# A two-layer mixture-of-experts network: shared experts moved, a softmax sum dropped, count stores on one queue

## The chip, the cores and the metric

The kernel runs on one core of a Trainium2 chip. A core has a matrix engine (PE, its weight loads shown as PEld), a vector engine (DVE), an activation engine (ACT), a general engine (POOL), a queue engine that only issues transfers (SP), and 16 DMA engines that all transfers share. Every engine works through its own instructions in order; semaphores order them between engines. The metric is the device time of one execution in microseconds (us).

## The reference

All values are float32. The input is 8192 tokens of 256 features (16 x 512 x 256). Four sublayers, each a layer norm and a residual sum: softmax attention, a mixture of experts (MoE), a recurrent attention with a forget gate, and the same MoE with the same weights again. The MoE is where the change lies:

```python
logits = x @ router_w.T                       # 64 experts
probs = softmax(logits)
topk_w, topk_ids = top_k(probs, 8)
topk_w = topk_w / sum(topk_w)                 # over the 8 chosen
# every token goes to its 8 experts; an expert takes its first 128 tokens
# in token order, later ones are dropped for it
pos = cumsum(onehot(topk_ids)) - 1
valid = pos < 128
# routed expert e, on its 128 tokens:
y = (silu(xb @ w_gate[e]) * (xb @ w_up[e])) @ w_down[e]        # 256 -> 192 -> 256
routed = sum over a token's valid experts of topk_w * y
# shared expert, on all tokens:
gu = x @ ws_gate_up
shared = (silu(gu[:, :192]) * gu[:, 192:]) @ ws_down
return routed + shared
```

## The kernel before

Tokens are worked on in 16 blocks of 512; a block is four chunks of 128 tokens, one token per partition. The profiled execution passes through these stages: attention of layer one (0 to 1378 us; the first MoE's block work is threaded into it, step by step, by the tables `dense` and `routed`, L425 to L450), the remainder of that block work and the first routed experts (to 1675), the forget attention (to 2151), the block loop of the second MoE (to about 2372), its routed experts (to 2627) and the last sum, `joined` (to 2672).

The order on each engine is written out: inside `manual_schedule` the instructions of PE, DVE, ACT, POOL and SP keep the order in which the program makes them. Transfers of a queue engine go through eight completion slots in turn, so that an issue can also wait for the landing of an older transfer that held its slot.

Class `Part` (L1388) holds the block work of one MoE. For block b: `normed` normalises the tokens and stores them to a DRAM table `rows` (L1520), from which the experts gather later; `features` transposes them to `xnT`; `logits` and `exps` give the unnormalised softmax `pr`; `choose` divides `pr` by its sum (its piece 0, L1564 to L1566), finds the eight largest (MAX8 and MATCH_REPLACE8, L1574 and L1575), and takes the chosen weights divided by their own sum, `wt` (L1581 to L1588); `count` transposes the 0/1 choice and makes a running count per expert with a scan, `cum` (L1596 to L1604). `added` and `counted` then store the counts to DRAM (L1607) and read them back as one row per chunk into the tile `cw` (L1493). The last block's counts go straight from tile to tile by four small transfers, `straight` (L1497 to L1501), alternately on SP and ACT.

The shared expert of a block is `gu` (12 PE passes into three banks, L1619), `silu` in two halves (a tanh on ACT, L1005, and two operations on DVE, L1006 and L1007, for each half), and `down` (16 PE passes, L1650, two copies on ACT, L1657, and one store of 512 KB by SP to the DRAM tensor `routed`, L1659). In the second MoE these run three blocks behind the choice (`lag = 3`, L1253 to L1273): iteration b does `gu` and `silu` of block b - 3 and `down` of block b - 4. In iterations 2 to 6 SP also fetches expert weights for five pairs of experts (`fetch`), 1.18 MB each time. The last three blocks' shared work lies behind the loop (L1275 to L1296), between the pieces of `place`, which turn the counts into token lists: `chunks_before` copies the last column of all counts into `after` (L1057), a product with a triangle sums the chunks (L1059), and for each pair of experts PE and DVE find the tokens (L1074 to L1103).

A routed expert e is: POOL gathers its 128 rows, `xe` (L1121, six experts ahead); PE transposes them (L1132), multiplies with the expert's weights (L1151) and after tanh and products with the down weights (L1175); ACT scales the result by the token's weight, `ye` (L1183); POOL adds it by an accumulating scatter to a DRAM tensor (L1186), even experts to `out`, odd ones to `routed`. Two tensors allow the next scatter to go while the last one lands. Weights come in pairs of experts into slots (11 pairs in the second MoE), POOL clearing each new slot once (L1465). At the end `joined` adds `routed` to `out` with eight accumulating transfers of 1 MB from POOL (L1369).

Of the kernel before, what the change touches and what calls it, by code (L numbers as in the profile page):

```python
# [17 lines left out]
P = 128  # L18
# [19 lines left out]
class Block:  # L38
# [129 lines left out]
    def attention(self, x, x1, wqkv, wo, rope, part, later):  # L168
# [11 lines left out]
        with ExitStack() as c:  # L180
# [270 lines left out]
            def each(s):  # L451

                n, i = divmod(s, CB)
                yield groups, n, weighted, i
                yield groups, n + 2, largest, i
                if i == 0:
                    yield groups, n - 1, summed
                    yield groups, n + 3, turn, kTs, H, "kT"
                if i == 1:
                    yield groups, n - 1, heads  # L460
                    yield groups, n + 1, row
                    yield groups, n + 3, turn, qTs, 0, "qT"
                b, at = divmod(s, steps)
                for work, far, *args in dense.get(at, []) + routed.get(at, []):

                    if b + far < z - 2 or work not in (part.shared, part.down):
                        yield self.nblk, b + far, work, *args

            with tc.manual_schedule(
# [540 lines left out]
    def routed(self, part, loads=False):  # L1010
# [9 lines left out]
        with ExitStack() as c:  # L1020
# [177 lines left out]
            with tc.manual_schedule(  # L1198
# [5 lines left out]
                    nc.sync.engine,  # L1204
                }
            ):
                nb, lag, ahead = self.nblk, 3, 6
                finds = {0: find(0, 2), 2: find(2, 2)}
                gathered = iter(range(E))

# [40 lines left out]
                    fetch(n)  # L1251

                if loads:  # L1253
                    for b in range(-4, nb + 1):
                        run(b + 4, nb, load)
                        if b == -3:
                            part.begin(nc.scalar)
                        run(b, nb, choose)
                        run(b + 2, nb, lambda b: part.normed(b, xs.pop(b)))
                        run(b + 1, nb, part.features)  # L1260
                        run(b - lag, nb, gu)
                        run(b - lag, nb, silu)
                        run(b + 1, nb, part.logits)
                        run(b + 1, nb, part.likely)
                        run(b, nb, part.count)
                        run(b, nb, counts)
                        run(b - 1 - lag, nb, down)
                        run(b + 1, nb, part.exps)
                        run(b + 3, nb, lambda b: part.moments(b, xs[b]))
                        if 2 <= b < 7:  # L1270
                            fetch(b - 2)
                        if b == nb:
                            chunks_before()  # L1273
                            place(0, 3)

                    begun, done, z = 5, 0, nb - 1
                    place(0, 2)
                    gather_to(1)
                    place(2, 3)
                    part.gu(z - 1, 0)  # L1280
                    place(2, 1)
                    part.gu(z - 1, 1)
                    place(2, 1)
                    gather_to(3)
                    silu(z - 1)
                    part.down(z - 2, 0)
                    part.down(z - 2, 2)
                    place(4, 3)
                    part.gu(z, 0)
                    place(4, 1)  # L1290
                    part.gu(z, 1)
                    place(4, 1)
                    gather_to(5)
                    silu(z)
                    down(z - 1)
                    down(z)  # L1296
                else:
                    begun, z = 8, nb - 1
                    room = part.own.enter_context(
# [38 lines left out]
                    place(8, 3)  # L1338
                    done = 2
                part.own.close()  # L1340
                part.slots(part.pairs - len(part.slot), "left")

                rest = [(n, piece) for n in range(begun, E // 2) for piece in range(4)]
                due, last = len(rest), E - 10
                for e in range(done - 2, E):
                    if e + ahead > 5:
                        run(e + ahead, E, gather_to)
                    place((e + 10) // many * many, 2 if (e + 10) % many == 0 else 1)
                    run(e + 2, E, turned)
                    run(e + 2, E, lastly)  # L1350
                    run(e + 1, E, widened)
                    run(e, E, narrowed)
                    while rest and (due - len(rest)) * last < due * (e + 1):
                        n, piece = rest[0]
                        if e < 2 * (n - part.pairs) + 3:
                            break
                        if piece == 0:
                            held(n)
                        part.fetch(*rest.pop(0))


    def joined(self, out, y):
# [25 lines left out]
class Part:  # L1388
# [3 lines left out]

    def __init__(self, ctx, k, x, y, weights, room, pairs, side):
        rw, self.w_gate, self.w_up, self.w_down, ws_gu, ws_down = weights
        self.ctx, self.pairs, self.slot, self.ws = ctx, pairs, [], {}
        self.k, self.nc, self.x, self.y, self.room = k, k.nc, x, y, room
        tc, T = k.tc, k.T
        self.own = ctx.enter_context(ExitStack())  # L1400
# [21 lines left out]
        self.bank = None  # L1422
        self.shared_weights = (rw, ws_gu, ws_down)

    def begin(self, queue):
        rw, ws_gu, ws_down = self.shared_weights
        nc, T, w = self.nc, self.k.T, self.pools[1]
        self.rw_sb = w.tile([P, KD, E], F32, name="rw_sb")
        queue.dma_start(out=self.rw_sb, in_=rw.rearrange("(k p) f -> p k f", p=P))

        self.wsg_sb = w.tile([P, KD, 2 * FF], F32, name="wsg_sb")
        for to, of, n in ((0, 0, FF), (FF, FF + P, FT), (2 * P, FF, P)):
# [7 lines left out]
        queue.dma_start(out=self.wsd_sb[0:FT, 1, :], in_=ws_down[P:FF, :])  # L1440

        self.hidden = []
        for i in range(self.room["hT"]):
            hT = w.tile([P, 2, BLK], F32, name=f"hT{i}")
            nc.gpsimd.memset(hT[FT:P, 1, :], 0.0)
            self.hidden.append(hT)
        for z in (self.rows, self.x, self.y):
            queue.dma_start(out=z[T : T + P, :], in_=self.k.zeros[:, 0 : z.shape[1]])


    def slots(self, n, side):
# [45 lines left out]
    def straight(self, b):  # L1497

        for i in range(CB):
            at, queue = b * CB + i, (self.nc.sync, self.nc.scalar)[i % 2]  # L1500
            queue.dma_start(out=self.cw[at : at + 1], in_=self.cum[:, ts(i, P)])  # L1501

    def tile(self, name, shape):
        return self.pools[self.room[name]].tile(shape, F32, name=name)
# [55 lines left out]
    def choose(self, b, piece):  # L1560
        nc, small, pr = self.nc, self.k.small, self.prs[b]
        if piece == 0:
            sm = small.tile([P, CB], F32, name="sm")
            nc.vector.tensor_reduce(sm, pr, AX.X, ALU.add)  # L1564
            nc.vector.reciprocal(sm, sm)
            nc.vector.tensor_tensor(  # L1566
                pr, pr, sm.unsqueeze(2).to_broadcast([P, CB, E]), ALU.mult
            )
            self.tops[b] = small.tile([P, CB, TOPK], F32, name="top")
            self.rests[b] = self.tile("rest", [P, CB, E])  # L1570
            return
# [39 lines left out]


    def gu(self, b, piece):
        nc, xnT = self.nc, self.xnTs[b]
        gu = self.gus[b, piece] = {}
        for m in ((0, 2), (1,))[piece]:
            gu[m] = self.bank()
            for kd in range(KD):
                nc.tensor.matmul(  # L1619
                    gu[m],  # L1620
                    lhsT=self.wsg_sb[:, kd, ts(m, P)],
                    rhs=xnT[:, kd, :],
                    start=(kd == 0),
                    stop=(kd == KD - 1),
                )
        if piece == 1:
            del self.xnTs[b]

    def silu(self, b, piece):
        if piece == 0:  # L1630
            self.hTs[b] = self.hidden[b % len(self.hidden)]
        gu = self.gus.pop((b, piece))
        high = (P, FT)[piece]
        gate = gu[piece][0:high]
        up = gu[2] if piece == 0 else gu[1][FT:P]
        th = self.tile("th", [P, BLK])[0:high]
        self.k.silu(self.hTs[b][0:high, piece, :], gate, up, th, 0.5)
# [5 lines left out]
    def down(self, b, i, pool=None):  # L1643
# [1 line left out]
        if i == 0:  # L1645
            self.ys[b] = (pool or self.pools[self.room["y"]]).tile([P, CB, D], F32, name="y")
        py = self.bank()
        for k in range(2):
            for m in range(2):
                nc.tensor.matmul(  # L1650
                    py[:, ts(k, D)],
                    lhsT=hT[:, m, ts(i + k, P)],
                    rhs=self.wsd_sb[:, m, :],
                    start=(m == 0),
                    stop=(m == 1),
                )
        nc.scalar.copy(self.ys[b][:, i : i + 2, :], py.rearrange("p (c d) -> p c d", c=2))  # L1657
        if i > 0:
            nc.sync.dma_start(  # L1659
                out=self.y[ts(b, BLK), :].rearrange("(c p) d -> p c d", p=P),  # L1660
                in_=self.ys.pop(b),
            )
            del self.hTs[b]


@with_exitstack
def hybrid_block_kernel(
# [27 lines left out]
    moe = (router, w_gate, w_up, w_down, ws_gu, ws_down)  # L1695
    later = k.forget_bias(b_bqk)
    with ExitStack() as c:
        part = Part(c, k, attended, routed, moe, ROOM, 13, "left")
        k.attention(x, attended, a_wqkv, a_wo, rope, part, later)
        k.routed(part)  # L1700
    k.forget_attention(
        attended, routed, out, (b_wqk, k.bqk_sb, b_wv, b_bv, b_wf, b_bf, b_wo, b_bo)
    )
    with ExitStack() as c:
        part = Part(c, k, out, routed, moe, ROOMY, 11, "left")
        k.routed(part, loads=True)
    k.joined(out, routed)

# [70 lines left out]
```

## Time and profile before

| what | value |
|---|---|
| device time, three runs | 2680.56, 2671.54, 2667.5 us; median 2671.54 |
| the profiled execution | 2674.27 us, span 2672.4 us |
| granted PE clock, mean | 0.95 |
| busy over the span | PE 92%, DVE 69%, ACT 48%, POOL 32% |
| transport | 226.48 MB, mean 85 GB/s |

The span is the time from the first to the last recorded instruction; the execution's own time has some two microseconds around it. A busy PE is not PE at its peak, since ends of matmuls are modelled. A group's line reads: line, engine, operation, output and input tile with their shapes, count, then busy time and mean duration in ns, then the idle time of the engine just before and what ended it. "x12" on a timeline's row means that twelve like instructions are drawn together. A trailing q (SPq, ACTq) is the engine's sequencer, which waits and issues transfers.

### The profile page before, as it was taken

The page shows a single profiled execution, that of the slowest core. Times are in us where ns is not written, and L with a number is a line of the kernel's source. Part 1 is how long each engine was busy: PE and PEld are TensorE (multiplying, and loading weights), DVE is VectorE, ACT ScalarE, POOL GpSimd, SP SyncE. Part 2 cuts the span into 40 slices and gives each one's busy share as a digit, 9 for nine tenths or more (in the row PEclk, how much of TensorE's full clock was granted, in tenths as well). Part 3 has the DMA queues.
Part 4 walks back from the last instruction along what each step waited for, and adds up shares of the span by engine and source line. Part 5 has one row for each costly group of instructions (what it writes and reads, how often), then busy time and mean ns, then how long its engine had stood idle before and what let it go on. Part 6 is the DMA issues. An engine that isn't in the chain of part 4 may idle for free.

```text
span 2672.4 us, 47696 instructions
## 1 busy us (share of the span) xinstructions
PE 2452.1 (92%) x17864; PEld 1517.9 (57%) x17864; DVE 1849.9 (69%) x4677; ACT 1293.0 (48%) x2654; POOL 845.6 (32%) x835
## 2 busy tenths in 40 slices
PE   6999999999999999999997886799999969998881
PEld 3444555445554455544446776567767656667771
DVE  6666667766777667776645664789889869966660
ACT  1656556565565655656542332466656523323330
POOL 3222212122121221212014776332332122117773
PEclk7999999999999999999898998899999969999996
DMA  1000111001110011100057887201111058739987
GB/s 57 2 17 19 35 37 35 21 21 35 37 35 21 21 35 37 35 21 13 27 151 207 237 229 156 90 29 58 60 53 53 21 146 185 175 106 258 246 220 148
DMA packets 210003, 226.48 MB, mean 85 GB/s; under 512 B 34286, under 2 KB 202222, under 8 KB 208750
## 3 DMA queue, kind: packets, MB, share of 16 engines
q1 hardware_dynamic: 180366, 174.43, 22.7%
q0 software_dynamic: 25728, 46.15, 8.7%
q8 instruction: 143, 2.34, 0.4%
q10 hardware_dynamic: 3680, 2.85, 0.3%
q14 instruction: 86, 0.70, 0.1%
HBM read 146.50 MB, written 84.48 MB: 86 GB/s over the span
## 4 chain that ended last, share of the span: by engine, by line
PE 76%; DVE 9%; DMA 7%; issue 3%; POOL 2%; ACT 1%; SPq 0%; ACTq 0%; POOLq 0%; DVEq 0%
PE sc L329 20%; PE sc L379 9%; DMA xe<-rows,token 5%; PE sc L255 4%; PE pb L797 4%; PE sc L1619 3%; PE sc L318 3%; PE sc L829 2%; PE sc L299 2%; PE sc L402 2%; PE sc L1650 2%; PE pb L861 2%; PE pb L906 2%; PE pb L722 2%; PE sc L1151 2%
## 5 line engine op out<-in xcount | busy, mean ns | idle before, releaser
L343 DVE TENSOR_REDUCE mx<-sc 128x1 f32<-128x512 f32 x1024 | 635.8, 684 | 375.5 <-PE sc L329 375.5
L369 ACT ACTIVATE pT<-sc 128x512 f32<-128x512 f32 x1024 | 528.6, 602 | 179.5 <-PE sc L329 179.5
L329 PE MATMUL sc<-qT,kT 17*128 17x512 f32 x2048 | 315.6, 646 | 0.0
L329 PE MATMUL sc<-kT,qT 16*128 16x512 f32 x2048 | 312.5, 609 | 1.5 <-DVE mx L343 1.4
L104 POOL TENSOR_SCALAR va<-mv 128x4 f32<-128x4 f32 x64 | 14.7, 230 | 756.6 <-DVE mv L98 742.8
L379 PE MATMUL sc<-pT,v 128*32 128x512 f32 x2048 | 241.8, 614 | 0.0
L846 DVE SCALAR_TENSOR_TENSOR pT<-sc,of,left 128x256 f32<-128x256 f32 x512 | 204.9, 474 | 23.2 <-PE sc L829 21.9
L329 PEld LDWEIGHTS sc<-kT,qT 16*128 16x128 f32 x2048 | 159.6, 189 | 94.3 <-issue 51.9
L277 POOL TENSOR_TENSOR t<-qk,rope_sb 128x512 f32<-128x512 f32 x62 | 78.8, 1271 | 404.1 <-ACT qk L263 396.9
L1121 POOL DMA_INDIRECT xe<-rows,token x128 | 131.0, 1023 | 96.8 <-DVE token L1103 39.7
L379 PEld LDWEIGHTS sc<-pT,v 128*32 128x32 f32 x2048 | 61.3, 112 | 173.1 <-issue 123.0
L329 PEld LDWEIGHTS sc<-qT,kT 17*128 17x128 f32 x2048 | 93.8, 184 | 90.0 <-issue 46.2
L255 PE MATMUL sc<-wqkv_sb,feat 128*128 128x512 f32 x256 | 128.0, 625 | 0.0
L144 ACT COPY oT<-sc 128x512 f32<-128x512 f32 x64 | 37.6, 587 | 169.4 <-PE sc L379 169.4
L797 PE MATMUL pb<-feat,wqk_sb 128*128 128x512 f32 x256 | 119.0, 598 | 0.0
L1186 POOL DMA_INDIRECT routed<-ye,token x64 | 101.9, 1592 | 41.2 <-ACT th L1160 10.4
L96 DVE BATCH_NORM_STATS2 bn<-x 128x6 f32<-128x256 f32 x256 | 89.1, 412 | 15.5 <-DMA x<-out 12.4
L318 PEld LDWEIGHTS sc<-ident,pad 128*128 128x128 f32 x512 | 54.8, 142 | 74.1 <-issue 38.9
L318 PE MATMUL sc<-ident,pad 128*128 128x128 f32 x512 | 86.1, 291 | 5.1 <-POOL pad L293 3.0
L285 POOL TENSOR_TENSOR t<-qk,rope_sb 128x256 f32<-128x256 f32 x124 | 90.7, 753 | 0.0
L1619 PE MATMUL sc<-xnT,wsg_sb 128*128 128x512 f32 x192 | 89.3, 603 | 0.0
L255 PEld LDWEIGHTS sc<-wqkv_sb,feat 128*128 128x128 f32 x256 | 45.8, 194 | 76.3 <-issue 38.3
(220 smaller groups left out, 4822.2 us busy)
## 6 DMA issues: line engine op xcount, KB each, us to landing
ws<-in_w_gate SPq DMA_DIRECT2D x64, 384.0 KB
ws<-in_w_up SPq DMA_DIRECT2D x64, 384.0 KB
rows<-xn SPq DMA_DIRECT2D x32, 512.0 KB
routed<-y SPq DMA_DIRECT2D x32, 512.0 KB
ws<-in_w_down SPq DMA_DIRECT2D x64, 256.0 KB
x<-in_x SPq DMA_DIRECT2D x16, 512.0 KB
attended<-x SPq DMA_DIRECT2D x16, 512.0 KB
ws<-in_w_down SPq DMA_DIRECT2D x64, 128.0 KB
```

The lines of the kernel that those rows point to most:

```text
L255: nc.tensor.matmul(pq, lhsT=xnTs[b][:, kd, ts(i, P)], rhs=wqkv_sb[:, kd, 0 : 2 * D], start=(kd == 0), stop=(kd == KD - 1),)
L285: eng.tensor_tensor(t2[:, :, lo : lo + HD // 2], qk2[:, :, :, 1 - half], rope_sb[:, i, HD + lo : HD + lo + HD // 2] .unsqueeze(1) .to_broa ...
L318: nc.tensor.transpose(pt[:, ts(i, P)], pads[b % 2][i][:, at : at + 4, :].rearrange("p h d -> p (h d)"), self.ident,)
L329: nc.tensor.matmul(scs[j], lhsT=lhs[at : at + high, ts(i, P)], rhs=rhs[at : at + high, :], start=True, stop=True,)
L343: nc.vector.tensor_reduce(mxs[n][:, j, i : i + 1], sc, AX.X, ALU.max, negate=True)
L369: nc.scalar.activation(pT[:, j, :], sc, AF.Exp, scale=float(HD) ** -0.5)
L379: nc.tensor.matmul(pav[ts(j, HP), :], lhsT=vs[b % 2][:, i, 4 * hg + j, :], rhs=pT[:, j, :], start=(i == 0), stop=(i == CB - 1),)
L797: nc.tensor.matmul(pq, lhsT=wqk_sb[:, kd, ts(m, P)], rhs=xnTs[b][:, kd, :], start=(kd == 0), stop=(kd == KD - 1),)
L846: nc.vector.scalar_tensor_tensor(pTs[n][:, :, ts(s8, HD)], sc[:, :, ts(s8, HD)], of[:, s8 : s8 + 1], here, ALU.mult, ALU.mult,)
L1121: nc.gpsimd.indirect_dma_start(out=xes[e], out_offset=None, in_=rows, in_offset=bass.IndirectOffsetOnAxis(ap=token[:, e : e + 1], axis=0),)
L1186: nc.gpsimd.indirect_dma_start(out=accs[e % 2], out_offset=bass.IndirectOffsetOnAxis(ap=token[:, e : e + 1], axis=0), in_=ye, in_offset=No ...
L1619: nc.tensor.matmul(gu[m], lhsT=self.wsg_sb[:, kd, ts(m, P)], rhs=xnT[:, kd, :], start=(kd == 0), stop=(kd == KD - 1),)
```

## The change

Five edits go together.

1. `choose` no longer divides by the softmax sum, in both MoEs. The chosen weights are divided by their own sum anyway, so the sum cancels.
2. In the second MoE the shared experts of blocks 3, 7 and 11 (`put_off`) leave the block loop. A generator, `between`, computes them in 24 pieces between the routed experts of e = 0 to 55: it loads the shared weights again (SP), loads the block's normalised rows from `rows` (SP), transposes them, and does the products in a pool of its own, `r_o`. A piece's second half (copies, tanh, products) follows at the start of the next expert. The results stay in three tiles until `paid` adds them to `out` with three accumulating transfers of 512 KB, ahead of `joined`. Since nothing else writes those blocks' rows of `routed`, `begin` clears them with twelve transfers of 128 KB on ACT's queue.
3. The other 13 blocks' shared work is cut into pieces with costs 4, 2, 2 and 2 and handed out evenly over the iterations (`shares`), from block 0 in iteration 0 on, in place of the fixed lag of three. Costs of 20 of 130, two blocks, are left for behind the loop.
4. `straight` issues its four transfers on ACT's queue alone, in both MoEs.
5. The second MoE has nine slots for pairs of weights instead of eleven.

```diff
@@ dense and routed tables of attention
-                    if b + far < z - 2 or work not in (part.shared, part.down):
+                    if work not in (part.shared, part.down) or (
+                        b + far < z - 2 and b + far not in part.put_off
+                    ):
@@ second layer's loop
-                    for b in range(-4, nb + 1):
+                    own = [b for b in range(nb) if b not in part.put_off]
+                    def first_part(b):
+                        part.gu(b, 0)
+                        part.silu(b, 0)
+                    def second_part(b):
+                        part.gu(b, 1)
+                        part.silu(b, 1)
+                    pieces = []
+                    for n, b in enumerate([*own, None]):
+                        if b is not None:
+                            pieces.append((4, b, first_part, b))
+                        if n > 0:
+                            pieces.append((2, own[n - 1], part.down, own[n - 1], 0))
+                            pieces.append((2, own[n - 1], part.down, own[n - 1], 2))
+                        if b is not None:
+                            pieces.append((2, b, second_part, b))
+                    total, spent = 10 * len(own), 0
...
+                    for b in range(-4, nb):
                         run(b + 4, nb, load)
                         if b == -3:
                             part.begin(nc.scalar)
                         run(b, nb, choose)
                         run(b + 2, nb, lambda b: part.normed(b, xs.pop(b)))
                         run(b + 1, nb, part.features)
-                        run(b - lag, nb, gu)
-                        run(b - lag, nb, silu)
+                        shares((total - 20) * (b + 1) // nb, b)
                         run(b + 1, nb, part.logits)
                         run(b + 1, nb, part.likely)
                         run(b, nb, part.count)
                         run(b, nb, counts)
-                        run(b - 1 - lag, nb, down)
                         run(b + 1, nb, part.exps)
                         run(b + 3, nb, lambda b: part.moments(b, xs[b]))
                         if 2 <= b < 7:
                             fetch(b - 2)
-                        if b == nb:
-                            chunks_before()
-                            place(0, 3)
-                    begun, done, z = 5, 0, nb - 1
+                    begun, done = 5, 0
+                    shares(total - 10)
+                    chunks_before()
+                    place(0, 3)
+                    shares(total - 8)
                     place(0, 2)
                     gather_to(1)
                     place(2, 3)
-                    part.gu(z - 1, 0)
...
+                    shares(total - 6)
+                    place(2, 2)
                     gather_to(3)
...
                     place(4, 3)
...
+                    shares(total - 4)
+                    place(4, 2)
                     gather_to(5)
+                    shares(total)
@@ routed experts
                 part.own.close()
+                filler = part.between("left") if part.put_off else iter(())
+                next(filler, None)
                 part.slots(part.pairs - len(part.slot), "left")
+                all_pieces, begun_pieces, open_piece = 8 * len(part.put_off), 0, False
...
                 for e in range(done - 2, E):
+                    if open_piece:
+                        next(filler, None)
+                        open_piece = False
...
                     run(e, E, narrowed)
+                    if e >= 0 and begun_pieces * (E - 8) < all_pieces * (e + 1):
+                        next(filler, None)
+                        open_piece = begun_pieces % 8 > 0
+                        begun_pieces += 1
...
+                for _ in filler:
+                    pass
+                part.paid()
@@ Part.begin
+        for b in self.put_off:
+            for i in range(CB):
+                at = b * BLK + i * P
+                queue.dma_start(out=self.y[at : at + P, :], in_=self.k.zeros[:, 0:D])
@@ Part.straight
-            at, queue = b * CB + i, (self.nc.sync, self.nc.scalar)[i % 2]
-            queue.dma_start(out=self.cw[at : at + 1], in_=self.cum[:, ts(i, P)])
+            at = b * CB + i
+            self.nc.scalar.dma_start(out=self.cw[at : at + 1], in_=self.cum[:, ts(i, P)])
@@ Part.choose
-            sm = small.tile([P, CB], F32, name="sm")
-            nc.vector.tensor_reduce(sm, pr, AX.X, ALU.add)
-            nc.vector.reciprocal(sm, sm)
-            nc.vector.tensor_tensor(
-                pr, pr, sm.unsqueeze(2).to_broadcast([P, CB, E]), ALU.mult
-            )
@@ new in Part
+    def between(self, side):
+        nc = self.nc
+        pool = ... tile_pool(name="r_o", bufs=1, side=side, reuse_waits="tile")
+        self.shared_from(pool, nc.sync, 1)
+        hT = self.hidden[0]
+        yield
+        for b in self.put_off:
+            here = slice(b * BLK, (b + 1) * BLK)
+            xn = pool.tile([P, CB, D], F32, name="xn_o")
+            nc.sync.dma_start(out=xn, in_=self.rows[here, 0:D]...)
+            yield
+            xnT = self.xnTs[b] = pool.tile([P, KD, BLK], F32, name="xnT_o")
+            for kd in range(KD):
+                (four transposes into a bank); yield; (copy by ACT); yield
+            th = pool.tile([P, BLK], F32, name="th_o")
+            for m in (0, 2, 1):
+                gu = self.bank()
+                self.chunk(b, m, gu)
+                yield
+                (tanh on ACT, products on DVE)
+                yield
+            y = pool.tile([P, CB, D], F32, name=f"y_o{b}")
+            self.owed.append((here, y))
+            for i in (0, 2):
+                py = self.bank()
+                self.lowered(py, hT, i)
+                yield
+                nc.scalar.copy(y[:, i : i + 2, :], ...)
+                yield
+
+    def paid(self):
+        for here, y in self.owed:
+            self.nc.gpsimd.dma_start(
+                out=self.x[here, :].rearrange("(p c) d -> p c d", c=CB),
+                in_=y,
+                accum_op=ALU.add,
+            )
@@ the second layer's Part
-        part = Part(c, k, out, routed, moe, ROOMY, 11, "left")
+        part = Part(c, k, out, routed, moe, ROOMY, 9, "left", (3, 7, 11))
```

## The prediction

> **What bounds the kernel now.** I read the times by windows first (one row for each stage), then what each queue waits for inside the second layer, then the groups of instructions by line, then the timeline at the seams. Nearly everything that changes lies between 2151 us, where the second layer's blocks start, and the end at 2672.4 us. Columns of the windows: stretch and length, busy time of PE, PEld, DVE, ACT and POOL with instructions, PE's granted clock, share of the DMA engines, GB/s.
> ```profile
> 2171.50:2182.00 10.50, 8.82 (x38) 6.89 (x36) 9.97 (x38) 2.92 (x7) 2.61 (x4) 0.50 0.47 141
> 2228.50:2360.50 132.00, 123.75 (x577) 87.66 (x576) 120.95 (x400) 41.85 (x80) 26.11 (x40) 0.99 0.73 174
> 2372.00:2400.00 28.00, 26.54 (x98) 17.47 (x99) 16.43 (x37) 6.69 (x13) 7.56 (x10) 0.94 0.26 83
> 2400.00:2440.00 40.00, 38.44 (x271) 34.50 (x270) 29.17 (x83) 14.49 (x38) 28.24 (x24) 1.00 0.89 248
> 2440.00:2600.00 160.00, 133.36 (x882) 117.43 (x881) 101.52 (x286) 51.83 (x135) 117.90 (x89) 0.96 0.92 241
> 2627.00:2672.00 45.00, 0.00 (x0) 0.00 (x0) 0.00 (x0) 0.00 (x0) 6.83 (x8) 0.50 0.91 186
> ```
> See four regimes. The block loop has DVE and PE both over 90% busy; its scans of the counts stand 12.57 us apart for most blocks, which is DVE's work for one block. The seam 2372 to 2400 is PE alone. The routed experts have no full engine, but a full transport (0.92). The end is DMA only.
>
> In the loop a third thing runs close behind: SP's queue. It stores a block's counts, must wait until they have landed, and only then issues what follows (the waits of SP, 2151 to 2372):
> ```profile
> SPq L1493 <- DMA counts<-cum: 68.3, 15, 5.9
> SPq L1501 <- DMA cw<-cum: 7.7, 1, 7.7
> ```
> By the timeline SP's counts stores start at 2201.64 (block 2), 2275.21 (block 7) and 2352.35 (block 14). While expert weights are fetched (blocks 2 to 6) SP takes some 16 us per block and falls 10.9 us behind DVE's scan of block 8; afterwards it takes 11.0 to 11.3 and catches up, to 1.3 us at block 13.
>
> The seam, from the timeline (start, duration, engine):
> ```profile
> 2360.57 1.19 ACTq L1501 DMA_DIRECT2D cw<-cum  x2
> 2360.89 5.31 PE L1619 MATMUL pb<-xnT,wsg_sb 128*128 128x512 f32 x12
> 2366.04 3.62 PE L1650 MATMUL pb<-wsd_sb,hT 128*128 128x256 f32 x16
> 2367.10 1.14 SPq L1501 DMA_DIRECT2D cw<-cum  x2
> 2371.34 0.22 DVE L1057 COPY after<-cw 64x64 f32<-64x64 f32 x1 [3.07 <-DMA routed<-y]
> ```
> See that ACT's two stores of the last counts go out at once, SP's two 6.5 us later, and the copy of all counts, on which every gather hangs, 4.2 us after those. PE does shared experts meanwhile and afterwards: a block costs 5.31 + 3.62 = 8.9 us.
>
> The routed experts, on POOL's timeline:
> ```profile
> 2398.60 1.91 POOL L1465 MEMSET ws<- 64x512 f32 x4 [4.30 <-PE pb L1650]
> 2405.35 1.64 POOL L1186 DMA_INDIRECT out<-ye,token  x1 [1.08 <-ACT ye L1183]
> 2407.30 0.99 POOL L1121 DMA_INDIRECT xe<-rows,token  x1 [0.31 <-issue]
> 2408.59 1.60 POOL L1186 DMA_INDIRECT routed<-ye,token  x1 [0.30 <-issue]
> ```
> One gather and one scatter are .99 + .30 + 1.6 + .30 = 3.19 us of POOL; the scatters run from 2405.35 (expert 0) to 2606.42 (expert 56), 3.59 us each. Never does it catch up, so the time of the first scatter carries through to the end.
>
> **The change, part by part**, against the profiled execution (2674.27 us, span 2672.4).
>
> 1. Softmax sum. Per block L1564, L1565 and L1566 leave DVE:
> ```profile
> L1564 DVE TENSOR_REDUCE sm<-pr 128x4 f32<-128x256 f32 x13 | 5.0, 386 | 0.7 <-ACT pr L1558 0.7
> L1566 DVE TENSOR_TENSOR pr<-pr,sm 128x256 f32<-128x256 f32 x13 | 5.5, 426 | 0.4
> L1007 DVE SCALAR_TENSOR_TENSOR hT<-th,pb 128x512 f32<-128x512 f32 (+1 forms) x26 | 17.9, 689 | 2.2 <-PE pb L1650 0.5
> ```
> .386 + .178 + .426 is .99, 1.09 with its gaps; 17.4 us in sixteen blocks. In the first layer that lies under attention with PE 98% busy: nothing there, and if that cover went it would be a gain.
>
> 2. Shared work in the loop. The build's order of instructions has 23 of DVE's half-block silu pairs (.689 + .676 = 1.37 us) up to the last scan, against 26 before: 4.1 us less. DVE alone could then scan block 15 at 2359.3 − 17.4 − 4.1, some 2338, or with its 3.4 us of waits gone 2334. The other side is SP. The new early silu halves (2, 1, 2 in iterations 0 to 2, where there was none) delay the scan of block 2: 5 × 1.37 − 3 × 1.09 is 3.6, about 1.5 of the zero stores' 7 us (1.5 MB at 212 GB/s) falls among the first loads, and I add .4 of the 1.1 by which the loop's first products, begun at half clock, were slower than 5.31 (6.40 at 2203); counts store 2 goes to 2207. (The twelve zero stores of 128 KB on ACT's queue cost it 12 × .35 to .59, 4 to 7 us after 2156.7; ACT's first need is 2166.8, so they fit, unless their slots wait for loads: then up to 3 us, in the range.) Blocks 2 to 7 are SP's, with the same 1.18 MB of weights per block: 73.6 us again. Blocks 7 to 14 take 7 × 11.2 less three y stores of 2.4 us (512 KB at 212 GB/s), 71. So counts 14 goes out at 2351.7, as before. The DVE gain is swallowed by SP. I take SP's value, because its landing wait is present in all 15 blocks; DVE's stays as the other end. PE's shared work shrinks by three blocks of 8.9 us and doesn't set this.
>
> 3. Last counts. ACT issues all four: 2.4 us instead of 1.19, ahead of its tanh, no wait for SP's slots. The copy of all counts then comes when counts 14 are in: 2351.7 + 5.75 (store to read-back issue, as before: 2352.35 to 2358.10) + 3.2 = 2360.7, or, if DVE's end holds, 2334 + 1.3 + 2.4 + 3.2 = 2341. Before: 2371.34. Parts 2 and 3 together: **−10.6** (−30 to −4). Queued behind ACT's two extra issues are one tanh and PE's down product, which now is not on the path. In the first layer it is: there both pairs went out at 1400.61 and ACT's tanh waited, so +1.4, less up to 1.1 from part 1: **+0.5** (−2 to +2.5).
>
> The Trainium skill's page "DMA: Bandwidth & Descriptors", section "Issuing engines are not separate DMA queues", says that issuing on several engines only saves the issuing time, and so speaks against part 3: by it, leaving SP costs two issues, +1.2 us instead of a gain. The row above with SP's pair 6.5 us late speaks for the gain, because a queue here also holds its own older waits.
>
> 4. The seam. Before, 27.0 us lie between the copy of counts and the first turned expert at 2398.32; PE's shared passes fill 12.8 + 10.7 = 23.5 of them by the groups in that stretch. After, one block's 8.9 us remains. The placement of the first pairs needs 4.5 us to the first gather and about 5 for its landing (the chain shows 5 to 7 per gather), so not under 10; I take 15. **−12** (−15 to −6). POOL's clearing of weight slots and the sixth gather move with it, since L1465 waited for PE's last L1650; next in line are the gathers themselves.
>
> 5. Fillers between routed experts. Three blocks: 3 × (8.9 + eight transposes of .28) = 33.4 us of PE in 55 experts, .61 each. PE's own share is 133.36/160 × 3.59 = 2.99, so 3.60 against a period of 3.59. DMA: 3 × 512 KB of normalised rows again and 576 KB of weights, 2.1 MB on some 50 MB, 4%. Bounds: below, nothing: in 2400 to 2440 PE was 96% busy and the scatters still ran at 3.62. Above, all of PE's time on the path: +33. PE at 97% gives 3.71, .12 × 55: **+7** (0 to +20), nearest the 96% row, which is this same stage. Two slots of weights fewer: by the pace that the loop sets, pairs are still asked for some nine experts, 32 us, before use, so nothing. POOL's queue has only the one clearing more.
>
> 6. Payment at the end. Three accumulating stores of 512 KB. The eight of 1 MB take 45 us, so 8.4; some of it lies beside the last routed scatter's landing, 2622.99 to 2627: **+5.5** (0 to +8.4). The order is serial by pairs (second, fourth and sixth joined store wait for one each), behind stores that are long already.
>
> Sum: −10.6 + .5 − 12 + 7 + 5.5 = −9.6, so 2664.7 on the profiled execution. That one lies 2.7 us above the median of the runs shown (2671.54), so 2662 in its terms.
>
> The first shared products now run at 2170, at a granted clock of 0.50. The skill's page "TensorE: Matmul & The Clock Gate", Part 1, has full clock after some 3.4 us of sustained work; the first row above (8.82 of 10.5 us busy, still 0.50) shows that here it did not come, since the work had gaps. By the rule the .4 us in part 2 would vanish; nothing else moves.
>
> **Rivals.**
> - SP does not hold the loop and DVE's gain arrives: parts 2 and 3 at −25 to −30, a total of −24 to −29, 2643 to 2648. For it: in the weight blocks DVE waited for its x tile only 3.4 us. Against it: 68.3 us of landing waits.
> - Slower: the fillers stop the chain. The routed stage has PE, ACT and POOL in orders written out by hand; a filler's copies and products stand ahead of the next expert's. If 33 us of PE come on top, with DMA at 0.92 unable to recover, the sum is −9.6 − 7 + 33 = +16, 2688. It decides at a growth above 30 us for slower by 0.5%, 17 for no gain. Against it: scatters ran 2.5 to 7 us behind their ready rows, which absorbs one filler.
> - The work is only moved: seam and loop give 16, stage and payment take it back (stage +13, payment +5.5): within 3 us of 2671.
>
> **How the numbers follow.** 0.5%, 13.4 us, is about what a measurement of this kernel can tell from no change. Forecast (SP's loop; 2652 to 2669): 0.45. DVE's gain arrives: 0.25. Slower: 0.16. Only moved: 0.14. Faster by over 0.5% (under 2658.2) takes the second case and some 0.2 of the first: 0.45; slower 0.16; the rest 0.39. The range leaves out the far ends of the second and third case: 2637 to 2686.
>
> **What would show it.** Right: the counts copy near 2361 with four ACT issues in a row, counts 14 near 2352 while DVE has idle time before its x tiles; first scatter 22 us before 2405; scatters 3.7 us apart; joined stores starting 5.5 us after the last scatter's landing. Wrong: scans every 10 us to the end (first rival); PE waiting on banks or scatters over 4 us apart (second); the first scatter after 2390 (third, or a seam that waits for reloaded weights).

## The result and the profile after

The changed kernel takes 2683.59 us (median of 4 runs, 2678.48 to 2687.4) beside 2670.46 for the kernel before: a ratio of 1.0043, 95% interval 1.0026 to 1.0060. It is slower by 0.43%, some 11 us, where 9.6 us of gain were forecast. The profiled execution of the changed kernel (2678.48 us, span 2676.4) is the fastest of its four and the one of before is 3.8 us above its median, so the two traces differ by 4 us only. What follows from the traces accounts for these 4; the rest of the difference lies in executions without a trace. The changed kernel itself has only these four executions; the kernel before, taken again beside each group of experiments, had medians from 2672.72 to 2678.01 us, which is why the experiments are compared by their ratios.

| step (from the timelines) | before | after | difference | forecast |
|---|---|---|---|---|
| first scan of the counts, at | 2180.9 | 2181.7 | +0.8 | +0.5 |
| first to last scan (the block loop) | 178.3 | 178.5 | +0.2 | these two: |
| last scan to the copy of all counts | 12.1 | 14.3 | +2.2 | -10.6 |
| copy to the first turned expert | 27.0 | 17.3 | -9.7 | -12 |
| that to the first scatter | 7.0 | 7.6 | +0.6 | 0 |
| first to last scatter | 217.6 | 221.4 | +3.8 | +7 |
| last scatter to the end | 49.4 | 55.6 | +6.2 | +5.5 |
| sum | | | +4.1 | -9.6 |

Five rows came near to their forecast. The loop and the last counts did not. The changed kernel's times by windows, columns as before:

```profile
2203.00:2360.00 157.00, 132.99 (x579) 92.28 (x578) 124.26 (x434) 44.52 (x86) 31.34 (x48) 0.88 0.79 169
2360.00:2374.50 14.50, 8.07 (x26) 4.51 (x24) 3.98 (x6) 2.17 (x5) 0.00 (x0) 0.94 0.40 100
2440.00:2600.00 160.00, 149.79 (x985) 129.63 (x983) 107.49 (x298) 60.82 (x151) 114.77 (x88) 1.00 0.92 243
```

In the loop DVE was busy 92% of the time before and is busy 79% now, PE 94% and now 85%: both have been relieved, and the loop is as long as it was. The second row holds the last counts: for 14.5 us PE is busy 8.1, DVE 4.0 and ACT 2.2. In the routed stage PE rose from 83% to 94%, and it cost little.

What SP waited for in the changed kernel's second layer (total, times, longest):

```profile
SPq L1540 <- DMA counts<-cum: 71.2, 15, 7.2
SPq L1697 <- ACT y L1695: 11.0, 3, 9.1
SPq L1567 <- DMA x<-out: 6.6, 1, 6.6
```

And what DVE waited for, in the same stretch:

```profile
DVE bn L96 <- DMA x<-out: 19.8, 4, 7.2
DVE th L1008 <- ACT th L1007: 10.2, 1, 10.2
DVE mx L1598 <- PE pb L1586: 5.8, 3, 4.8
```

In the kernel before, the first of these was:

```profile
DVE bn L96 <- DMA x<-out: 12.4, 3, 9.0
```

The wait of SP for the landing of the counts is still there, 71 us, and DVE's gain has turned for the most part into waiting for x tiles: from 2203 to 2360 alone these waits grew from 3.4 to 19.8 us, while DVE's busy time shrank from 144.7 to 124.3. The loads of x stand in SP's order behind the landing wait. The last counts, from the timeline of ACT and SP:

```profile
2361.47 8.53 ACTq L1548 DMA_DIRECT2D cw<-cum  x4
2370.04 1.07 ACT L1695 COPY y<-pb 128x512 f32<-128x512 f32 x2 [9.91 <-DMA cw<-cum]
2371.00 1.08 ACT L1007 ACTIVATE th<-pb 64x512 f32<-64x512 f32 x2
```

SP's rows at the same time:

```profile
2360.65 0.27 SPq L1540 DMA_DIRECT2D cw<-counts  x1
2361.47 10.03 SPq L1697 DMA_DIRECT2D routed<-y  x2
```

ACT's four issues take 8.53 us where 2.4 were forecast, and two copies and two tanh stand behind them, for which DVE waits (the 10.2 above) and then PE. The trace keeps for each instruction the semaphores that it waits for, and for each transfer the one on which it counts its landing, its slot. By these, the first three issues find slots whose transfers have landed, and are out by 2364.1. The fourth has the slot of ACT's own first: that one lands at 2369.5, and the fourth goes out then. The chain of work that ended last has the same wait:

```profile
2361.47 8.03 DMA cw<-cum
```

### The profile page after: what moved, and what is told of

Read it like the earlier page. It is cut to its first block, busy times and chain, and to the rows that moved or that the text cites. A ratio compares the mean times of both kernels' runs of the same rounds, so it can differ in the third digit from the quotient of the medians.

```text
span 2676.4 us, 47702 instructions
## 1 busy us (share of the span) xinstructions
PE 2448.6 (91%) x17888; PEld 1515.0 (57%) x17888; DVE 1818.6 (68%) x4581; ACT 1296.2 (48%) x2660; POOL 846.9 (32%) x838
## 4 chain that ended last, share of the span: by engine, by line
PE 76%; DMA 10%; DVE 8%; issue 2%; POOL 1%; ACT 1%; SPq 0%; POOLq 0%; ACTq 0%; DVEq 0%
PE sc L329 20%; PE sc L379 9%; PE sc L255 4%; DMA xe<-rows,token 4%; PE pb L799 4%; PE sc L1666 3%; PE sc L318 3%; PE sc L831 2%; PE sc L299 2%; PE sc L402 2%; PE sc L1707 2%; PE pb L863 2%; PE pb L908 2%; PE pb L724 2%; DMA routed<-ye,token 2%
## 5 line engine op out<-in xcount | busy, mean ns | idle before, releaser
L369 ACT ACTIVATE pT<-sc 128x512 f32<-128x512 f32 x1024 | 528.6, 602 | 179.6 <-PE sc L329 179.5
```

The source lines that it names most:

```text
L369: nc.scalar.activation(pT[:, j, :], sc, AF.Exp, scale=float(HD) ** -0.5)
```

## The experiments

First to last scan, last scan to copy, and the ratio to the kernel before, for all of them:

| kernel | loop, us | to copy, us | ratio (95%) |
|---|---|---|---|
| before | 178.3 | 12.1 | 1 |
| sum dropped, alone | 175.8 | 13.0 | 0.9997 (0.9980 to 1.0014) |
| one queue, alone | 178.5 | 9.1 | 0.9999 (0.9984 to 1.0013) |
| spread by pieces, alone | 193.5 | 9.2 | 1.0006 (0.9991 to 1.0020) |
| changed, no block put off | 191.0 | 8.5 | 1.0021 (1.0005 to 1.0036) |
| changed, two queues | 179.1 | 12.6 | 1.0022 (1.0008 to 1.0037) |
| changed | 178.5 | 14.3 | 1.0043 (1.0026 to 1.0060) |
| before, late read-back | 174.6 | 8.9 | 0.9978 (0.9966 to 0.9991) |
| changed, none put off, late read-back | 178.5 | 8.6 | 0.9971 (0.9956 to 0.9986) |
| changed, late read-back | 159.2 | 10.6 | 0.9938 (0.9916 to 0.9960) |
| the same, two queues | 159.5 | 9.5 | 0.9937 (0.9911 to 0.9963) |
| the same, logits first | 166.2 | 10.6 | 0.9955 (0.9938 to 0.9972) |
| changed, y stores by ACT | 194.0 | 15.1 | 1.0076 (1.0059 to 1.0093) |
| that, late read-back | 179.5 | 9.8 | 1.0011 (0.9993 to 1.0029) |

The theory: SP's wait for the landing of the counts holds the loop, and completion slots shared between queues stretch the last counts. Rivals: DVE holds the loop, or the volume of transport does.

**Softmax sum alone.** The three DVE operations of `choose` are taken out of the kernel before.

```diff
-            sm = small.tile([P, CB], F32, name="sm")
-            nc.vector.tensor_reduce(sm, pr, AX.X, ALU.add)
-            nc.vector.reciprocal(sm, sm)
-            nc.vector.tensor_tensor(pr, pr, sm.unsqueeze(2)..., ALU.mult)
```

> The kernel before without the softmax sum (part 1 alone). Theory: DVE gives up 17 us in the second layer's loop but SP's wait for the landing of the counts holds the blocks; in the kernel before SP was 1.3 us behind DVE at the end, so the last scan comes at most 6 us earlier: 0 to 6 us faster than before, 2664 to 2671. Rival: DVE is the bound alone: 14 to 18 us faster, near 2654.

Measured 2672.43 beside 2672.72: no difference. The scans of blocks 2 to 6 stand 11.49 us apart instead of 12.57, DVE's saving to the letter; then intervals of 14.8, 15.5 and 16.6 us give most of it back, and 2.5 us of 17 are left at the end. DVE as the only bound is excluded.

**Late read-back.** On the changed kernel, SP reads a block's counts one iteration later:

```diff
-                    part.added(b, stored=b < nb - 1)
-                    (part.counted if b < nb - 1 else part.straight)(b)
+                    if b > 0:
+                        part.counted(b - 1)
+                    part.added(b, stored=b < nb - 1)
+                    if b == nb - 1:
+                        part.straight(b)
```

> The changed kernel with one move: SP reads a block's counts back one iteration later, just ahead of the next block's counts store, so that it no longer stands still until the store has landed. Theory: that wait (71 us in 15 blocks) is what swallowed DVE's gain; without it the last scan comes at 2338 to 2345 instead of 2360, and the time falls by 10 to 20 us, to 2663 to 2673. Rival: what holds the loop is the volume of transport (0.78 of the DMA engines), and the issue merely waits elsewhere: the last scan moves by less than 5 us and the time by less than 5.

Measured 2655.96 us (6 runs, 2653.12 to 2657.5), the last scan at 2343.4. The loop shrinks by 19.3 us. SP's waits in that kernel's second layer and the last counts:

```profile
SPq L1633 <- POOL wt L1630: 31.1, 9, 5.5
SPq L1652 <- DVE bn L96: 17.6, 6, 4.6
SPq L1543 <- DMA counts<-cum: 13.8, 5, 4.2
```

Its last counts, from ACT's timeline:

```profile
2344.75 2.48 ACTq L1551 DMA_DIRECT2D cw<-cum  x4
```

The landing wait falls from 71.2 to 13.8 us, and SP now waits for the engines that make its data, which is how it should stand. Much the same bytes move in a shorter time (194 GB/s from 2203 to 2344 instead of 169), so the volume was not the bound. The four issues take 2.48 us, as was forecast: here their four slots held only transfers that had landed.

On the kernel before, the same edit:

> The kernel before with the counts read back one iteration later in the second layer, nothing else. Theory: in the kernel before DVE and SP stood almost level at the end of the loop, DVE with 12.57 us of work per block; so the move alone gives only DVE's few waits: first to last scan 173 to 178 us instead of 178.3, the whole 0 to 8 us faster, 2664 to 2672. Rival: SP's landing wait was the bound of the kernel before as well, and the move alone gives what it gave on the changed kernel: 17 us or more, near 2655.

Measured 2666.72, ratio 0.9978. The scans stand 12.57 us apart from block 2 to block 13 with one interval of 12.9: there DVE does hold the loop, as the forecast read it. Between the two kernels with late read-back (0.9978 and 0.9938, intervals that do not touch) the change is worth 0.4%, some 11 us: the gain that was forecast for it, once SP is out of the way.

**No block put off.**

```diff
-        part = Part(c, k, out, routed, moe, ROOMY, 9, "left", (3, 7, 11))
+        part = Part(c, k, out, routed, moe, ROOMY, 9, "left", ())
```

> The changed kernel with no block put off (part 2 undone; spread, sum, one queue and nine slots stay). Theory: the payment's 6.2 us at the end and the 3.8 us by which the routed stage grew go, 10 us back; against them three more y stores of 2.4 us and 8 us of DVE in a loop that SP holds, so that the last scan comes 5 to 9 us later: within 4 us of the changed kernel. Rival: the loop is held by DVE, so the last scan comes 8 us later and the time is the same or slower by up to 4; second rival: the loop has room, the last scan does not move, and 10 us are gained.

> The changed kernel with the late read-back and no block put off (all sixteen blocks' shared experts spread in the loop). Theory: with SP out of the way DVE's work counts, 11.5 us per block: first to last scan 168 to 174 us against 159.2 with three blocks put off; the payment (6 us) and the growth of the routed stage (4 us) go. So 2655 to 2662: putting off pays for itself by no more than a few us. Rival: without the three blocks' relief PE and DVE together take over 178 us for the loop as in the run without put-off blocks (191): slower than 2668.

Measured 2677.7 and, with late read-back, 2664.05. The first is 6 us under the changed kernel by the ratios, a little more than the 4 expected: its loop is 12.5 us longer, and the end has the 45.1 us of before again. The intervals of 1.0021 and 1.0043 overlap, so what putting off costs in the changed kernel isn't settled. With late read-back the loop is 178.5 us without put-off blocks and 159.2 with them, and the time 2 us above what was expected. The 168 to 174 that DVE's work alone would give were missed (DVE waits 13.5 us for logits there), for a reason that the next run shows.

**Spread alone.** The kernel before with `shares` in place of the lag of three, all sixteen blocks in the loop; sum, queues and slots as before.

```diff
-                        run(b - lag, nb, gu)
-                        run(b - lag, nb, silu)
+                        shares((total - 20) * (b + 1) // nb, b)
...
-                        run(b - 1 - lag, nb, down)
...
```

> The kernel before with its sixteen blocks' shared experts handed out by pieces from iteration 0 on, instead of with a lag of three; no other part of the change. Theory: the pieces stand directly ahead of the logits and use products of the same iteration, so PE and DVE wait for each other where the lag of three had kept them apart (13.2 us of DVE for logits in the run without put-off blocks): first to last scan 188 to 196 us against 178.3, the seam gives back 8 to 10 since less is left behind the loop; total 0 to 8 us slower than before, 2672 to 2681. Rival: the loop was longer in that run by reason of the dropped sum or SP alone, and the spread costs nothing: 178 to 181 us between scans, and 8 to 10 us faster by the seam.

Measured 2676.84 beside 2675.85, and 193.5 us of loop, 15 more than before; the seam gives it back. What DVE waited for from 2161 to 2385 in this kernel:

```profile
DVE mx L1598 <- PE pb L1586: 14.8, 6, 4.8
```

And in the kernel before, to 2372:

```profile
DVE mx L1551 <- PE pb L1539: 0.3, 1, 0.3
```

This is a new wait that the forecast did not have: DVE's maximum of the logits waits behind shared products that the same iteration put ahead of them on PE, and PE waits in turn for `hT` (16.8 us in 4 waits). With a lag of three neither happened. With three blocks put off there is less of it (5.8 us).

**Logits first.** On the changed kernel with late read-back the iteration's pieces go behind `logits` and `likely`.

```diff
-                        shares((total - 20) * (b + 1) // nb, b)
                         run(b + 1, nb, part.logits)
                         run(b + 1, nb, part.likely)
+                        shares((total - 20) * (b + 1) // nb, b)
                         run(b, nb, part.count)
```

> The changed kernel with the late read-back, and the shared pieces of an iteration behind the logits and their reduction instead of ahead of them. Theory: with SP free, DVE holds the loop and still waits 5.8 us for logits that stand behind shared products on PE; with the order turned these waits go, and first to last scan takes 152 to 157 us instead of 159.2: 2649 to 2655. Rival: the products then come later and DVE waits for them instead (for the tanh halves), or PE for DVE's choice: 158 to 164 us, within 3 us of 2656 or slower.

Measured 2665.88, ratio 0.9955, loop 166.2 us: the rival, and more than its 158 to 164. That the loop is longer by 7 us is clear in the traces; the ratio's interval overlaps that of the run with logits last. DVE's waits for logits are 0.3 us now, but it waits 11.9 us for tanh halves (4.2 in one wait before) and 6.8 for the transposed choice (0.9 before).

**Two queues for the last counts.** `straight` alternates between SP and ACT again.

```diff
-            self.nc.scalar.dma_start(out=self.cw[at : at + 1], in_=...)
+            queue = (self.nc.sync, self.nc.scalar)[i % 2]
+            queue.dma_start(out=self.cw[at : at + 1], in_=...)
```

> The changed kernel with the last counts again on SP and ACT in turn (part 4 undone, both layers). Theory: completion slots are shared by all queues, so the four issues on ACT alone took 8.5 us and everything behind them on ACT waited; undone, the copy of all counts follows the last scan by some 10.8 us as before instead of 14.3, ACT's waiting copies come at once and PE does its rest of shared work meanwhile: 4 to 8 us faster than the changed kernel, some 2676 to 2680. Rival: what the issues wait for is transport still under way, which SP's two would wait for as well: within 2 us of the changed kernel.

> The changed kernel with the late read-back and the last counts on SP and ACT in turn. Theory: with the reads done early the slots that ACT's four issues need are free (they took 2.5 us in the run with the late read-back, 8.5 in the changed kernel), while SP's two would stand behind SP's own older transfers: 0 to 5 us slower than with one queue, 2656 to 2661. Rival: one queue costs here as well, 4 to 6 us faster, near 2651.

> The kernel before with the last counts on ACT alone, in both layers. Theory: the completion slots are shared, so ACT's third and fourth issue wait for transfers of SP's queue and hold ACT's copies: the copy of all counts follows the last scan by 10 to 14 us (12.1 before), total within 4 us of before. Rival, the forecast's term: ACT's issues wait for nothing but the scan, the copy follows by 7 us, 5 us faster.

Undone in the changed kernel: 2679.16 us, ratio 1.0022 instead of 1.0043, 5.6 us by the ratios, though the intervals overlap. The last counts barely gain by it, since now SP's pair waits:

```profile
2366.97 1.20 ACTq L1548 DMA_DIRECT2D cw<-cum  x2
2367.41 8.27 SPq L1548 DMA_DIRECT2D cw<-cum  x2
```

The copy follows the scan by 12.6 instead of 14.3, and the first scatter follows the last scan by 39.2 us in both traces. So the rival fits the traces, and the 5.6 us are not shown to come from the queue. By the semaphores SP's second issue here has the slot of ACT's first, as ACT's fourth has it in the changed kernel. With late read-back the number of queues makes no difference (2656.6). Alone on the kernel before, the issues went out at once:

```profile
2362.62 2.48 ACTq L1501 DMA_DIRECT2D cw<-cum  x4
```

The copy came 3 us sooner, and the time did not move (0.9999). My theory of waiting for slots did not hold there: the four had four slots, all of older transfers that had landed. The changed kernel with no block put off gives 2.48 us as well, without late read-back. So what counts is which slots the program's order hands to the four, not one queue as such.

**y stores by ACT.** In the second layer ACT issues the y stores that it makes, on the changed kernel and with late read-back.

```diff
-            nc.sync.dma_start(
+            (nc.scalar if self.put_off else nc.sync).dma_start(
                 out=self.y[ts(b, BLK), :]...
```

> The changed kernel with the second layer's y stores issued by ACT, which makes them, instead of SP; the counts are read back at once, as in the changed kernel. Theory: what holds SP is the landing wait of the counts (71 us), not the y stores (11 us of waits for ACT's copies): first to last scan 170 to 178 us against 178.5, total 0 to 6 us faster than the changed kernel, 2675 to 2682. Rival: it is the y stores just ahead of the counts stores that make SP late: 159 to 165 us between scans, as with the late read-back, 12 us or more faster.

> The changed kernel with the late read-back and the y stores on ACT. Theory: DVE's work holds the loop once SP is free, so nothing is left to win: first to last scan 158 to 161 us, within 3 us of 2656. Rival: SP's remaining waits (13.8 us for counts, 31 for the weights' rows) still cost: 4 to 8 us faster, 2648 to 2652.

Measured 2696.31 and 2677.3; by the ratios 9 us and 19 us slower than the same kernels with SP's stores (the intervals of the first pair just touch, those of the second are far apart). Neither theory had this. SP's waits of the first of them:

```profile
SPq L1540 <- DMA counts<-cum: 41.1, 13, 6.8
SPq L1649 <- DMA routed<-y: 23.9, 3, 8.3
SPq L1528 <- DMA routed<-y: 16.2, 2, 13.7
SPq L1567 <- DMA routed<-y: 15.5, 2, 8.4
SPq L1630 <- DMA routed<-y: 8.9, 1, 8.9
```

SP's stores of counts, fetches of expert weights (L1528), rows and weights wait 64.5 us for y stores that ACT issued. A weight fetch shares no data with y; what it shares is the completion slot: by the semaphores both fetches wait for the one on which they themselves will count their landing, and which the y store still holds. That is the mechanism of the last counts seen from the other side.

## Why the prediction was wrong

The median of 2683.59 lies inside the range (2637 to 2686), on the side that was given 0.39 for no change and 0.16 for slower. That it lies inside is luck: the upper end was there for fillers that stop the chain, and they did not. Against the forecast's steps:

- **Part 1, sum:** right. Dropped alone it gives nothing (0.9997).
- **Part 2, the loop:** its conclusion was right and a consequence was left out. SP swallows DVE's gain: counts 14 was stored at 2354.3 (forecast 2351.7), and freeing SP brought 19.3 us. But I let the last scan run ahead of SP, to 2338 or earlier. It doesn't: x tiles come through the same queue, and the scan was at 2360.2, beside SP's read-back at 2360.65. The mutual waits of spread products and logits were not seen either (15 us of loop in the run with the spread alone); with three blocks put off 5.8 us of DVE's 14.8 for logits are left.
- **Part 3, last counts:** this is where the forecast failed: −10.6 for parts 2 and 3 together against +2.4 measured. The copy of all counts was to follow SP's read-back of counts 14, the last scan and its four issues being long over. It came at 2374.5 instead of 2360.7. Of these 13.8 us, 3.2 are the later read-back. The other 10.6 are the last counts, which now stood on the path. In the runs whose four issues took 2.48 us the copy comes 8.5 to 10.6 us after the scan, so by my estimate 5 to 7 of them come from the scan not being ahead, and the remaining 4 to 6 from the wait for a slot (8.53 us for four issues instead of 2.4), behind which ACT's copies and tanh, DVE and PE stood still. "No wait for SP's slots" named the wrong holder: the slot was ACT's own. I had misread the row `SPq L1501 <- DMA cw<-cum: 7.7` in the same way: there SP's first issue has the slot of ACT's first, so what it waited for was the landing of a last count, not an older transfer of SP. I had set that wait against the Trainium skill's page "DMA: Bandwidth & Descriptors", section "Issuing engines are not separate DMA queues". A change of queue doesn't remove it, and alone, moving the issues brought no time (0.9999), so the page's rule, that only issuing time is saved, came nearer than my reading.
- **Part 4, seam:** right, -9.7 against -12.
- **Part 5, fillers:** right in kind. +3.8 against +7: PE at 94% in the routed stage did not hold POOL's scatters, 3.51 us apart against 3.45 on average. The slower rival, fillers that stop the chain, did not happen.
- **Part 6, payment:** +6.2 against +5.5.

The changed kernel's end shows the payment, POOL's timeline:

```profile
2622.48 2.75 POOL L1775 DMA_DIRECT2D out<-y_o  x3 [0.15 <-issue]
2624.74 1.39 POOL L1405 DMA_DIRECT2D out<-routed  x1
2628.00 1.64 POOL L1405 DMA_DIRECT2D out<-routed  x2 [1.87 <-DMA out<-y_o]
```

In the kernel before the joined stores start with:

```profile
2627.34 6.83 POOL L1369 DMA_DIRECT2D out<-routed  x8 [2.79 <-DMA routed<-ye,token]
```

The first joined store starts 2.6 us earlier than in the kernel before and the end is 4.0 us later, so the three stores cost 6.6 us of transport between them, little of it hidden.

So the slowdown came by a way that no rival described. The sign did not turn on the fillers: the gain of the loop and the last counts did not arrive, while the payment (6.2) and the longer stage (3.8) did, against 9.7 from the seam. The third rival, that the work is only moved, comes nearest. Open is why the medians differ by 11 to 13 us where the traces differ by 4: no trace of a slower execution is at hand. The last counts' waits vary with the landing of transfers and may do it, but that was only argued. Some of it may lie ahead of the loop: the kernel before and the same with late read-back share all code up to there, and their first scans stand 6 us apart (2180.9 and 2187.0).

## What to carry to other kernels

Before relieving the busiest engine, look for a queue that waits for the landing of its own store: everything behind it in order, loads included, is paced by it, and its price only shows once the engine is faster. Reading back one iteration later cost five lines and was worth 0.2% alone and 1% on the changed kernel. Moving an issue, or anything that shifts the order of issues, changes which older transfers it waits for, so the slots have to be looked up before such a move is called free.

## What was unexpected of the hardware

- The y stores on ACT's queue held SP's unrelated issues for 64.5 us in all; the two queues were not independent, since they share completion slots. Even four issues of one queue in a row are not safe: the fourth can have the slot of the first.
- PE's clock rose earlier. From 2171.5 to 2182 the changed kernel's row is:

```profile
2171.50:2182.00 10.50, 10.50 (x45) 6.58 (x44) 9.99 (x37) 3.31 (x7) 2.61 (x4) 0.84 0.49 153
```

With PE busy without a gap (10.50 of 10.5) the granted clock was 0.84, and 1.00 in the row after it (2182 to 2192), where before 8.82 of 10.5 left it at 0.50. That agrees with what the Trainium skill's page "TensorE: Matmul & The Clock Gate", Part 1, says of sustained work. It did not spare the first shared product, which started at 2172.0 and still took 6.72 us instead of 5.31, so the .4 us of part 2 did not vanish. Nor do busy time and gaps alone decide, as the forecast had it: in the kernel before with late read-back PE was busy 10.15 of the same 10.5 us, 4.9 of them (2174.3 to 2179.3) without a gap, and the clock stayed at 0.50. Its work there was transposes and the narrow products of the logits only; whether that is the reason is not shown.
